# A message-passing layer on one core: coarser loads of edge features, destinations, empty rows and late rows, and the last three stores on another queue

## The chip, the core and the metric

The kernel runs on one core of a Trainium2 chip. It is written by hand, engine by engine: TensorE (PE; its weight loads are listed apart as PEld), VectorE (DVE), ScalarE (ACT), GpSimd (POOL) and SyncE (SP), which here does nothing but issue DMAs. The metric is the device time of one execution in microseconds (us); smaller is better. An execution's time is a little longer than the span from its first to its last instruction in the profile.

## What is computed

100,000 edges join 6,250 nodes of 128 numbers each. For each edge the rows of both ends and the edge's own 128 features are multiplied by a weight of 384 x 128, normalized over the 128 outputs, scaled, passed through relu, and summed at the edge's source node. The sum is added to the node's row and normalized again. The edges come sorted by destination, the sum goes by source.

```python
x = x + gnn(x, [src, dst], edge_attr); return layernorm(x)
# gnn:
msg_in = concatenate([x[row], x[col], edge_attr], axis=-1)   # row = src, col = dst
h = msg_in @ W + b                                           # W: 384 x 128
mu = mean(h, -1);  var = mean(square(h - mu), -1)
h = (h - mu) * rsqrt(var + 1e-5) * gamma + beta
out = segment_sum(relu(h), row, num_segments=6250)
```

## The kernel before

**Tiles, pieces, slots.** The edges are cut into 782 tiles of 128 (`TILES`), and four tiles (`PT = 4`) make a piece: 196 pieces. The main loop goes through the pieces in order, one piece per turn; a turn is called a slot here. The tiles are also divided into six splits of 168, 168, 168, 120, 80 and 78 tiles (`SPLITS`), each with a table `sorted` of its own in HBM.

**First half of a piece** (by destination). PE multiplies the four tiles of features `eT` (128 x 128 floats each) by the third part of the weight (L611), then adds the destination's part: a one-hot matrix `ohd`, which DVE makes from the piece's destinations `db` (L599), times a window `win` of a table of projected nodes that the kernel has written to HBM itself (L615). ACT copies the result from `hp` to one of eight buffers `hs` (`evict`, L623), and POOL scatters its 512 rows with four indirect DMAs (L641) to the places in `sorted` at which rows of the same block of source nodes lie together. The scatters of a slot are issued one slot later or more, each tied to one of the matmuls of that slot, so that they go out spread over it.

**Second half** (by source). 50 blocks of 125 nodes (`NB`, `BN`) make 25 pairs in every split. A split's pairs are worked through while the next split's pieces run (`work`, `class Pair`): SP loads the pair's rows from `sorted` (`load_pair`, L715, into `hl`, the late rows; four buffers), DVE makes a one-hot `ohe` from them (L733, `ones`), PE turns it, ACT copies `hl` on (L755, `seed`), PE adds the source's part (L772, `pick`), ACT squares (L781), DVE scales and cuts (L796, `scale`), PE sums (L805, `sums`), and DVE adds to `acc` (L810). A pair has k = 2 x 4, 2 x 3 or 2 x 2 tiles by split (8 in the first three splits, 6, 4 and 4 in the last three); `KMAX` is 8. The pair's load is issued six steps ahead of its `ones`, where four steps make one pair. In a slot stand 2.4 steps in the first splits, 3.3 in split 3, and 5 from slot 161 on: there five pairs fall on four slots. The last split's pairs come after the last piece, as `Unit`s of two pairs (one at the ends), and then the layernorm of the nodes and the stores of the result (`Unit.end`, L954).

**Empty rows.** `sorted` has room for a fixed number of rows per block, more than are used. The unused end of each is filled with a row that counts for nothing, before a split's scatters begin: `clear` (L232), one DMA for each pair of blocks, issued one or two per slot in the last 26 or 30 slots before the split (in split 0 in its own first slots).

**Order.** The order of PE, DVE, ACT and SP is written out by hand: each executes its instructions as the program's text issues them. SP's order in a slot q is: `edge_loads(ahead)` with `ahead` running up to q + 4 (features, L141, then destinations, L573, both for two slots in even slots only; three buffers of each), `edge_window(ahead)` (a register load and the window, L585; six buffers), `clear_pairs`, and the late rows that fall due in the slot's steps. Each waits in this order, so one that waits for a buffer holds up all behind it on SP. With three buffers of two slots, the features for q + 4 and q + 5 go to the buffer that q - 2 and q - 1 have used, so their load waits for the products of q - 1.

**The end.** After the last store there is a branch on a flag (L1268) to a general path that is not taken in this execution; the instructions of that path stand in the program behind it. A hint in the program (L1228) tells all engines ahead of time which way the branch goes.

Of the kernel before, what the change touches and what calls it, by code (L numbers as in the profile page):

```python
# [16 lines left out]
P = 128  # L17
D = 128
# [31 lines left out]
PG_AT = 192  # L50
XG = 4
ROW = 132
ACW = 130
# [13 lines left out]
def dram_ap(t, offset, ap):  # L67
    return bass.AP(tensor=t.tensor, offset=t.offset + offset, ap=ap)
# [16 lines left out]
def fast_path(ctx, tc, io, bad_d, found):  # L85
# [45 lines left out]
    dst0_i = setup.tile([1, BY_PE, PT * P], I32, name="dst0_i")  # L131
    DG = 2
    held = {}

    def edge_feats(q):
        t0 = q * PT
        g = min(DG, PIECES - q)
        eT = edge.tile([P, DG * PT * P], F32, name="eT", bufs=3)
        for n in ([(0, g)] if q else [(i, 1) for i in range(g)]):
            c0, c1 = n[0] * PT * P, min((n[0] + n[1]) * PT * P, (TILES - t0) * P)  # L140
            nc.sync.dma_start(eT[:, c0:c1], io["eT"][:, t0 * P + c0:t0 * P + c1])  # L141
        held["eT", q // DG] = eT

# [418 lines left out]
    def edge_loads(q):  # L562

        if q % DG or q >= PIECES:
            return
        t0 = q * PT
        g = min(DG, PIECES - q)
        if ("eT", q // DG) not in held:
            edge_feats(q)
        db = edge.tile([P, DG * PT * P], BF16, name="db", bufs=3)  # L570
        if q >= BY_PE:
            c1 = g * PT * P
            nc.sync.dma_start(  # L573
                db[:, :c1], dram_ap(drel_d, t0 * P, [[0, P], [1, c1]]))
        held[q // DG] = (held.pop(("eT", q // DG)), db)

# [12 lines left out]
    def edge_hot(q):  # L589
        if q >= PIECES:  # L590
            return
        m = min(PT, TILES - q * PT)
        c0 = q % DG * PT * P
        db = held[q // DG][1][:, c0:c0 + m * P]
        if q < BY_PE:
            db = psum.tile([P, PT * P], F32, name="sel", bufs=BANKS["sel"])
            nc.tensor.matmul(db, ones_h[0:1, :], drel0[0:1, q, :], start=True, stop=True)
        oh = edge.tile([P, PT * P], BF16, name="ohd", bufs=3)
        nc.vector.tensor_scalar(oh[:, :m * P], db, part_w, None, op0=ALU.is_equal)  # L599
        held["oh", q] = oh  # L600

    def edges(s, q):
        t0 = q * PT
        m = min(PT, TILES - t0)
        c0 = q % DG * PT * P
        eT = held[q // DG][0][:, c0:c0 + m * P]
        oh, win = held.pop(("oh", q)), held.pop(("win", q))
# [101 lines left out]
    loaded = {}  # L709

    def load_pair(s, p):

        k = 2 * SPLITS[s][1]
        pair = late["blk"].tile([P, KMAX, ROW], F32, name="hl", bufs=4)
        nc.sync.dma_start(flat(pair[:, :k, :]),  # L715
                          dram_ap(sorted_d[s], p * k * P * ROW, [[k * ROW, P], [1, k * ROW]]))
        loaded[s, p] = pair

    class Pair:
# [8 lines left out]
        def ones(self):  # L728

            blk, k = late["blk"], self.k  # L730
            self.hl = loaded.pop((self.s, self.p))
            self.ohe = blk.tile([P, KMAX, P], F32, name="ohe", bufs=4)
            nc.vector.tensor_tensor(self.ohe[:, :k, :],  # L733
                                    self.hl[:, :k, D:D + 1].to_broadcast([P, k, P]),
                                    row_bc(iota_p, k), op=ALU.is_equal)
# [83 lines left out]
    class Unit:  # L819
# [7 lines left out]
        def load(self):  # L827
            self.hl = late["blk"].tile([P, KMAX, ROW], F32, name="hl", bufs=4)
            for i in range(self.n):
                j0 = i * self.kp  # L830
                nc.sync.dma_start(flat(self.hl[:, j0:j0 + self.kp, :]),
                                  dram_ap(sorted_d[self.s], (self.p0 + i) * self.kp * P * ROW,
                                          [[self.kp * ROW, P], [1, self.kp * ROW]]))

# [110 lines left out]
        def end(self, last=False):  # L945
# [8 lines left out]
            nc.sync.dma_start(io["out"][:, self.b0 * D:(self.b0 + m) * D], flat(y))  # L954

# [147 lines left out]

    cleared = {s: 0 for s in range(n_split)}

    def clear_pairs(s, n):
        for p0 in range(cleared[s], min(cleared[s] + n, NB // 2)):
            i = clear(s, p0, 1, nc.sync)
            if s == 0:
                tc.declare_no_dep(i.ins, group="early", reason="see check_early")  # L1110
                tc.add_to_no_dep_group("clear", i.ins)
            cleared[s] = p0 + 1

# [111 lines left out]
    for i in range(1, n - 1):  # L1225
        tail(i)
    tc.no_sync_barrier()
    tc.mark_branch_hint_location("general", "LikelyTaken", engines=(  # L1228
        mybir.EngineType.PE, mybir.EngineType.DVE, mybir.EngineType.Activation,
        mybir.EngineType.Pool, mybir.EngineType.SP))  # L1230
    a, b, c, d = units[-4:]
# [29 lines left out]
def gnn_resnorm_kernel(ctx, tc, io):  # L1261
# [3 lines left out]
    with ExitStack() as inner:  # L1265
        found = []
        fast_path(inner, tc, io, bad_t, found)
    with tc.If(found[0] > 0, preferred_fallthrough_block=True, label="general"):  # L1268
        with ExitStack() as inner:
            general_path(inner, tc, io)  # L1270
# [233 lines left out]
```

## Time and profile before

| what | value |
|---|---|
| median of three runs | 1375.33 us (1369.01, 1375.33, 1378.67) |
| profiled execution | 1380.69 us, span 1378.9 us |
| mean granted TensorE clock | 0.857 of full speed |
| DMA | 128,052 packets, 247.22 MB, 179 GB/s over the span |
| of these on SP's and ACT's queue (q1) | 101,924 packets, 191.92 MB, 46.8% of 16 engines' span |
| POOL's scatters (q0) | 25,104 packets, 53.05 MB, 11.0% |

One execution was profiled, and all durations below are of that one; it was 5.4 us longer than the median. In a row of a group, `x782: 867/971/1241, 19.9 to 1274.6` means 782 instructions of min/median/max 867, 971 and 1241 ns, of which the first began at 19.9 us and the last at 1274.6 us of the span. A row of waits tells who waited for what, the total in us, how often, and the longest. In the timeline a row begins with the start and the time from the first to the last end of its group (`x2`: two instructions). An engine's name with a q behind it is its sequencer: `SPq` is SP issuing DMAs. Bytes: a load for two slots of features is 512 KB, of destinations 256 KB (read once for each of the 128 partitions), a pair's late rows are 528 KB, 396 KB or 264 KB, its empty rows 198 KB or 132 KB.

### The profile page before, as it was taken

What the parts mean: (1) busy time and instruction counts of PE and PEld (TensorE: products, weight loads), DVE (VectorE), ACT (ScalarE), POOL (GpSimd) and SP (SyncE); (2) the same over time, 40 slices, a digit from 0 to 9 for tenths busy, and PEclk for the clock granted to TensorE, in tenths of its full rate; (3) what the DMA queues carried; (4) which work ended last, traced back from release to release, by engine and by line L of the source; (5) the groups of instructions that cost most, each with busy time, mean ns of one, the idle gap of its engine ahead of it and who ended that gap; (6) DMA issues with size and microseconds to landing.
All of it is one profiled execution on the core that took longest, in us unless ns stands there. A gap on an engine that the chain in (4) does not pass through costs nothing. (4 is left out here: it accounts for less than half of the span.)

```text
span 1378.9 us, 27543 instructions
## 1 busy us (share of the span) xinstructions
PE 975.2 (71%) x8886; PEld 870.3 (63%) x8886; DVE 855.0 (62%) x2376; ACT 773.5 (56%) x3118; POOL 798.9 (58%) x835
## 2 busy tenths in 40 slices
PE   7457464345767676778777677778778787876895
PEld 5445453334666665777676667777778776765674
DVE  8573434524465656556575657678688867554797
ACT  4223232112555655564565557676778788665796
POOL 3656666666566665666565666566555555556054
PEclk9768687666888989878888899999999999988898
DMA  7758586455666655556656555665667655543332
GB/s 223 236 168 255 171 241 204 142 154 155 184 199 210 199 158 163 178 157 198 207 171 200 172 184 178 208 208 187 190 193 227 183 181 171 170 140 100 112 122 72
DMA packets 128052, 247.22 MB, mean 179 GB/s; under 512 B 47005, under 2 KB 61231, under 8 KB 127897
## 3 DMA queue, kind: packets, MB, share of 16 engines
q1 hardware_dynamic: 101924, 191.92, 46.8%
q0 software_dynamic: 25104, 53.05, 11.0%
q8 instruction: 71, 1.16, 0.4%
q14 instruction: 83, 0.68, 0.2%
q10 hardware_dynamic: 870, 0.40, 0.1%
HBM read 155.49 MB, written 89.80 MB: 178 GB/s over the span
## 5 line engine op out<-in xcount | busy, mean ns | idle before, releaser
L641 POOL DMA_INDIRECT sorted<-hs,place_i x782 | 760.4, 972 | 498.1 <-issue 210.6
L772 PE MATMUL sel<-xa,ohn 128*128 128x128 bf16 x2550 | 214.3, 232 | 174.9 <-issue 78.5
L781 ACT ACTIVATE sq<-sel 128x128 f32<-128x128 f32 x850 | 224.2, 280 | 158.9 <-PE sel L772 58.2
L772 PEld LDWEIGHTS <-ohn 128*128 128x128 bf16 x2550 | 174.8, 104 | 204.4 <-issue 174.7
L611 PE MATMUL hp<-w,eT 128*128 128x128 f32 x1564 | 258.3, 314 | 51.2 <-issue 37.9
L611 PEld LDWEIGHTS hp<-w,eT 128*128 128x128 f32 x1564 | 234.3, 225 | 83.2 <-issue 59.3
L805 PE MATMUL pa<-msg,ohe 128*128 128x130 f32 x1700 | 259.2, 308 | 24.1 <-issue 14.9
L623 ACT COPY hs<-hp 128x512 f32<-128x512 f32 x196 | 114.2, 583 | 288.7 <-issue 97.7
L805 PEld LDWEIGHTS pa<-msg,ohe 128*128 128x128 f32 x1700 | 236.4, 217 | 32.2 <-issue 19.0
L796 DVE SCALAR_TENSOR_TENSOR msg<-sel,rstd,cut 128x128 f32<-128x128 f32 x850 | 240.7, 345 | 8.0
L781 ACT ACTIVATION_READ_ACCUMULATOR sq<-sel 128x1 f32 x850 | 178.8, 210 | 0.0
L810 DVE TENSOR_TENSOR acc<-acc,pa 128x260 f32<-128x260 f32 x125 | 53.0, 424 | 201.0 <-PE pa L805 57.9
L733 DVE TENSOR_TENSOR ohe<-hl,beside 128x1024 f32<-128x1024 f32 (+2 forms) x125 | 131.4, 1052 | 23.3 <-PE sel L772 14.6
L749 ACT COPY ohn<-tr 128x1024 bf16<-128x1024 bf16 (+2 forms) x125 | 109.5, 876 | 37.9 <-PE pa L805 14.7
L755 ACT COPY sel<-hl 128x512 f32<-128x512 f32 (+1 forms) x225 | 127.9, 569 | 1.8 <-DVE msg L796 1.0
L599 DVE TENSOR_SCALAR ohd<-db,part_w 128x512 bf16<-128x512 bf16 x192 | 69.7, 363 | 72.1 <-remote 50.9
L615 PE MATMUL hp<-win,ohd 126*128 126x128 bf16 x782 | 88.5, 236 | 17.4 <-issue 15.4
L790 DVE RECIPROCAL rstd<-std 128x4 f32<-128x4 f32 (+1 forms) x225 | 38.6, 171 | 96.7 <-ACT std L784 45.2
L615 PEld LDWEIGHTS <-ohd 126*128 126x128 bf16 x782 | 69.0, 108 | 25.2 <-issue 20.9
L745 PE MATMUL tr<-ident_h,ohe 128*128 128x128 bf16 x850 | 75.5, 230 | 11.1 <-issue 9.4
L784 ACT ACTIVATE std<-ss,eps 128x4 f32<-128x4 f32 (+1 forms) x225 | 66.9, 297 | 7.3
L745 PEld LDWEIGHTS <-ohe 128*128 128x128 bf16 x850 | 57.7, 103 | 14.3 <-issue 14.2
(198 smaller groups left out, 1043.4 us busy)
## 6 DMA issues: line engine op xcount, KB each, us to landing
eT<-in_eT SPq DMA_DIRECT2D x96, 512.0 KB
hl<-sorted SPq DMA_DIRECT2D x75, 528.0 KB
db<-drel_d SPq DMA_DIRECT2D x96, 256.0 KB
sorted<-empty SPq DMA_DIRECT2D x100, 198.0 KB
hl<-sorted SPq DMA_DIRECT2D x50, 264.0 KB
sorted<-hs,place_i POOLq DMA_INDIRECT x782
hl<-sorted SPq DMA_DIRECT2D x25, 396.0 KB
sorted<-empty SPq DMA_DIRECT2D x50, 132.0 KB
```

The lines of the kernel that those rows point to most:

```text
L611: pe(nc.tensor.matmul(hp[:, j, :], eT[:, at], w[:, 2, :], start=j == 0, stop=False, skip_group_check=True), 4)
L615: pe(nc.tensor.matmul(hp[:, j, :], oh[:3 * WN, at], win[:3 * WN, :], start=False, stop=j == m - 1, skip_group_check=True))
L623: nc.scalar.copy(hs[:, :m, 0:D], hp[:, :m, :])
L641: i = nc.gpsimd.indirect_dma_start(out=sorted_d[s][:, :], out_offset=bass.IndirectOffsetOnAxis(ap=place_i[:parts, t:t + 1], axis=0), in_=h ...
L733: nc.vector.tensor_tensor(self.ohe[:, :k, :], self.hl[:, :k, D:D + 1].to_broadcast([P, k, P]), row_bc(iota_p, k), op=ALU.is_equal)
L745: pe(nc.tensor.transpose(tr[:, j, :], half[:, j0 + j, 1::2], ident_h))
L749: nc.scalar.copy(self.ohn[:, :self.k, :], self.tr[:, :self.k, :])
L755: nc.scalar.copy(self.sel[g][:, :m, :], self.hl[:, j0:j0 + m, 0:D])
L772: pe(nc.tensor.matmul(sel[:, j, :], self.ohn[:, j0 + j, :], xa[:, b, i * D:(i + 1) * D], start=False, stop=j == m - 1 and i == 2, skip_gro ...
L781: nc.scalar.activation(sq[:, j, :], self.sel[g][:, j, :], AF.Square, accum_out=ss[:, j:j + 1])
L796: nc.vector.scalar_tensor_tensor(self.msg[:, j0 + j, 0:D], self.sel[g][:, j, :], rstd[:, j:j + 1], cut, op0=ALU.mult, op1=ALU.max)
L805: pe(nc.tensor.matmul(self.pa[:, h, :], self.ohe[:, j, :], self.msg[:, j, :], start=(j == h), stop=(j == k - 2 + h)), 4)
```

## The change

Four kinds of transfers are cut anew, and three stores change queues. Nothing that is computed changes.

- **Features**: one load brings three slots instead of two (768 KB), in two buffers instead of three. The first group keeps two slots; the others begin at slots 2, 5, 8 and so on. So the group that begins at q + 4 goes to the buffer of q - 2, q - 1 and q, and its load, issued in slot q as before, waits for that slot's own products.
- **Destinations**: one load brings five slots instead of two (640 KB), two buffers instead of three; groups begin at 4, 9, 14 and so on. Groups of three and of five meet in every fifteenth slot.
- **Empty rows**: one DMA clears five pairs (two in split 0), when that many have fallen due.
- **Late rows**: where a pair has four tiles (the last two splits), one DMA brings two pairs, at the place where the first of the two is due; the buffer always had room for eight tiles.
- **Last stores**: the three stores of the last three units go on ACT's queue instead of SP's.
- **Branch**: the hint and a barrier ahead of it are gone, and the path that is taken is no longer the one that falls through.

```diff
@@
+EG, DG = 3, 5
+CLEAR = (2, 5, 5, 5, 5, 5)
...
-    DG = 2
     held = {}
+
+    def feats_from(q):
+        return 0 if q < 2 else q - (q - 2) % EG
 
     def edge_feats(q):
         t0 = q * PT
-        g = min(DG, PIECES - q)
-        eT = edge.tile([P, DG * PT * P], F32, name="eT", bufs=3)
+        g = min(EG, PIECES - q) if q else 2
+        eT = edge.tile([P, EG * PT * P], F32, name="eT", bufs=2)
         for n in ([(0, g)] if q else [(i, 1) for i in range(g)]):
             c0, c1 = n[0] * PT * P, min((n[0] + n[1]) * PT * P, (TILES - t0) * P)
             nc.sync.dma_start(eT[:, c0:c1], io["eT"][:, t0 * P + c0:t0 * P + c1])
-        held["eT", q // DG] = eT
+        held["eT", q] = eT
...
     def edge_loads(q):
-        if q % DG or q >= PIECES:
+        if q >= PIECES:
             return
-        t0 = q * PT
-        g = min(DG, PIECES - q)
-        if ("eT", q // DG) not in held:
+        if feats_from(q) == q and ("eT", q) not in held:
             edge_feats(q)
-        db = edge.tile([P, DG * PT * P], BF16, name="db", bufs=3)
-        if q >= BY_PE:
-            c1 = g * PT * P
+        if q >= BY_PE and (q - BY_PE) % DG == 0:
+            c1 = min(DG, PIECES - q) * PT * P
+            db = edge.tile([P, DG * PT * P], BF16, name="db", bufs=2)
             nc.sync.dma_start(
-                db[:, :c1], dram_ap(drel_d, t0 * P, [[0, P], [1, c1]]))
-        held[q // DG] = (held.pop(("eT", q // DG)), db)
+                db[:, :c1], dram_ap(drel_d, q * PT * P, [[0, P], [1, c1]]))
+            held["db", q] = db
...
+    def load_rows(s, p, n):
+        k = 2 * SPLITS[s][1]
+        rows = late["blk"].tile([P, KMAX, ROW], F32, name="hl", bufs=4)
+        nc.sync.dma_start(rows[:, :n * k, :].rearrange("p (n k) d -> p n (k d)", n=n),
+                          dram_ap(sorted_d[s], p * k * P * ROW,
+                                  [[k * ROW, P], [k * P * ROW, n], [1, k * ROW]]))
+        return rows
+
     def load_pair(s, p):
 
         k = 2 * SPLITS[s][1]
-        pair = late["blk"].tile([P, KMAX, ROW], F32, name="hl", bufs=4)
-        nc.sync.dma_start(flat(pair[:, :k, :]),
-                          dram_ap(sorted_d[s], p * k * P * ROW, [[k * ROW, P], [1, k * ROW]]))
-        loaded[s, p] = pair
+        n = KMAX // k
+        if p % n:
+            return
+        pair = load_rows(s, p, min(n, NB // 2 - p))
+        for i in range(n):
+            loaded[s, p + i] = pair, i * k
...
         def load(self):
-            self.hl = late["blk"].tile([P, KMAX, ROW], F32, name="hl", bufs=4)
-            for i in range(self.n):
...
+            self.hl = load_rows(self.s, self.p0, self.n)
...
-            nc.sync.dma_start(io["out"][:, self.b0 * D:(self.b0 + m) * D], flat(y))
+            queue = nc.scalar if last else nc.sync
+            queue.dma_start(io["out"][:, self.b0 * D:(self.b0 + m) * D], flat(y))
...
     cleared = {s: 0 for s in range(n_split)}
+    wanted = dict(cleared)
 
     def clear_pairs(s, n):
-        for p0 in range(cleared[s], min(cleared[s] + n, NB // 2)):
-            i = clear(s, p0, 1, nc.sync)
+        wanted[s] = min(wanted[s] + n, NB // 2)
+        while cleared[s] < wanted[s]:
+            m = min(CLEAR[s], NB // 2 - cleared[s])
+            if wanted[s] < cleared[s] + m:
+                break
+            i = clear(s, cleared[s], m, nc.sync)
...
-    tc.no_sync_barrier()
-    tc.mark_branch_hint_location("general", "LikelyTaken", engines=(
...
-    with tc.If(found[0] > 0, preferred_fallthrough_block=True, label="general"):
+    with tc.If(found[0] > 0, preferred_fallthrough_block=False):
```

Two places show how this moves instructions. The first is SP around the load of the features for piece 188, near the end of the pieces, where the slots hold most steps: eT are features, db destinations, win a window (with the register load and the address ahead of it), hl late rows. Before:

```order
L715 DMA hl_14253<-sorted4_75 128x528
L715 DMA hl_14312<-sorted4_75 128x528
L141 DMA eT_14329<-in_eT 128x1024
L573 DMA db_14331<-drel_d_70 128x1024
L581 TENSOR_LOAD base_c_177
L585 ISA
L585 DMA win_14336<-xb_d2_69 126x1x128
L715 DMA hl_14383<-sorted4_75 128x528
L715 DMA hl_14428<-sorted4_75 128x528
```

Now:

```order
L718 DMA hl_14022<-sorted4_75 128x2x528
L145 DMA eT_14039<-in_eT 128x1536
L583 TENSOR_LOAD base_c_177
L587 ISA
L587 DMA win_14044<-xb_d2_69 126x1x128
L718 DMA hl_14134<-sorted4_75 128x2x528
L575 DMA db_14140<-drel_d_70 128x2560
```

The two single loads of late rows ahead of the features have become one double load, and so have the two behind the window; the pair that the second of the single loads ahead of the features brought now comes with the load behind the window. The destinations have moved out of their place behind the features to one behind the late rows, since their groups no longer begin in the same slots.

The second place is ACT's end, from its last work on (sq and fstd belong to the last unit's variance). Before:

```order
L931 ACTIVATE sq,var<-y,total 128x128 x2
L934 ACTIVATE fstd<-var,eps 128x2
L1268 COMPARE_AND_BRANCH
L1300 DMA g_wn<-in_W 128x2x128
L1302 DMA g_we<-in_W 128x128
```

Now:

```order
L941 ACTIVATE sq,var<-y,total 128x128 x2
L944 ACTIVATE fstd<-var,eps 128x2
L965 DMA out<-y 128x512
L965 DMA out<-y 128x256 x2
L1280 COMPARE_AND_BRANCH
L1280 UNCONDITIONAL_BRANCH
```

Three stores stand between ACT's last work and the branch, and behind the branch there is now an unconditional one. The loads at L1300 and L1302, which followed the branch before, belong to the general path and are not executed. On SP the three stores are gone from the same place.

More of the change, by code (lines that the diff above doesn't have):

```diff
@@ L592, in edge_hot @@
         m = min(PT, TILES - q * PT)
-        c0 = q % DG * PT * P
-        db = held[q // DG][1][:, c0:c0 + m * P]
-        if q < BY_PE:
+        if q >= BY_PE:
+            c0 = (q - BY_PE) % DG * PT * P
+            db = held["db", q - (q - BY_PE) % DG][:, c0:c0 + m * P]
+        else:
             db = psum.tile([P, PT * P], F32, name="sel", bufs=BANKS["sel"])
@@ L604, in edges @@
         m = min(PT, TILES - t0)
-        c0 = q % DG * PT * P
-        eT = held[q // DG][0][:, c0:c0 + m * P]
+        q0 = feats_from(q)
+        c0 = (q - q0) * PT * P
+        eT = held["eT", q0][:, c0:c0 + m * P]
         oh, win = held.pop(("oh", q)), held.pop(("win", q))
@@ L730, in ones @@
             blk, k = late["blk"], self.k
-            self.hl = loaded.pop((self.s, self.p))
+            rows, j0 = loaded.pop((self.s, self.p))
+            self.hl = rows[:, j0:j0 + k, :]
             self.ohe = blk.tile([P, KMAX, P], F32, name="ohe", bufs=4)
@@ L1111, in clear_pairs @@
                 tc.add_to_no_dep_group("clear", i.ins)
-            cleared[s] = p0 + 1
+            cleared[s] += m
     ahead = 3
@@ L1226, in fast_path @@
         tail(i)
-    tc.no_sync_barrier()
-    tc.mark_branch_hint_location("general", "LikelyTaken", engines=(
-        mybir.EngineType.PE, mybir.EngineType.DVE, mybir.EngineType.Activation,
-        mybir.EngineType.Pool, mybir.EngineType.SP))
     a, b, c, d = units[-4:]
```

4 lines of the change are left out of this document (removed).

## The prediction

> **What bounds the kernel now.** First the page's head and busy shares:
>
> ```profile
> span 1378.9 us, 27543 instructions
> ...
> PE 975.2 (71%) x8886; PEld 870.3 (63%) x8886; DVE 855.0 (62%) x2376; ACT 773.5 (56%) x3118; POOL 798.9 (58%) x835
> ```
>
> No engine is full, but POOL is nearer its limit than its share says. Its scatters with first and last start, its largest row in the view of waits, and the pieces' products on PE:
>
> ```profile
> L641 POOL DMA_INDIRECT sorted<-hs,place_i x782: 867/971/1241, 19.9 to 1274.6; - x196
> POOL sorted L641 <- issue: 210.6, 535, 3.4
> L611 PE MATMUL hp<-w,eT x1564: 269/275/582, 13.9 to 1264.6; 128*128 128x128 f32 x196
> ```
>
> 782 scatters at 0.971 us are 759 us, and 210.6 us of pauses in which POOL waits for nothing shown make 970 us of the 1255 us from 19.9 to 1274.6. The other 285 us are waits on others: the scatters are tied to the products of their slot. PE goes through 196 pieces in 1250.7 us, so a slot is 6.4 us, and POOL, PE, ACT and DVE share it in a ring. No load stands in that ring. The view of one source line lists who waited for it (us in total, times). For the features (L141) that is the first row below, for the windows (L585) the next two, for the late rows (L715) the last; for the destinations (L573) the list is empty:
>
> ```profile
>   PEld hp L611: 0.8, 1
>   PE hp L615: 1.2, 1
>   PEld hp L611: 0.4, 1
>   PE hp L615: 0.6, 1
> ```
>
> Those are 3 us of 1379. The other way round SP waits often, at the feature loads for PE to be done with a buffer and at the late rows for ACT (SP's own waits, the three longest):
>
> ```profile
> SPq L715 <- ACT sel L755: 120.6, 35, 11.9
> SPq L141 <- remote: 96.7, 18, 10.1
> SPq L141 <- PE sel L772: 92.6, 15, 10.5
> ```
>
> So SP runs ahead until buffers stop it. Fewer issues buy nothing directly; what counts is whether a coarser load still comes in time.
>
> **The parts.** *Issues.* One feature issue, min/median/max ns:
>
> ```profile
> L141 SPq DMA_DIRECT2D eT<-in_eT x99: 3/348/1353, 1.7 to 1229.1; - x99
> ```
>
> The program has 756 DMAs on SP before and 529 on SP plus 3 on ACT after: feature loads 99 to 67, destinations 96 to 39, empty rows 150 to 38, late rows 150 to 127, and three stores moved. That is 224 issues less; at 0.348 us 78 us of SP's time. SP is waited for by nobody, so I take 0; the other end, a gain, is a rival below. The bytes stay the same.
>
> *Features, three slots in two buffers.* Leads are shortest near the end of the edges, where five pairs fall on four slots. SP, PE and DVE there, and the row of that stage in the table of windows (us; busy of PE, PEld, DVE, ACT, POOL; clock, DMA share, GB/s):
>
> ```profile
> 1182.09 0.34 SPq L141 DMA_DIRECT2D eT<-in_eT  x1
> 1182.48 0.80 SPq L573 DMA_DIRECT2D db<-drel_d  x1
> 1184.01 0.81 SPq L585 DMA_DIRECT2D win<-xb_d  x1
> 1184.92 4.62 SPq L715 DMA_DIRECT2D hl<-sorted  x2
> 1180.50 1.11 PE L611 MATMUL hp<-w,eT 128*128 128x128 f32 x8
> ...
> 1189.57 1.91 PE L611 MATMUL hp<-w,eT 128*128 128x128 f32 x8
> ...
> 1216.50 1.05 PE L611 MATMUL hp<-w,eT 128*128 128x128 f32 x8
> 1199.87 0.68 DVE L733 TENSOR_TENSOR ohe<-hl,beside 128x512 f32<-128x512 f32 x1
> 1000.00:1250.00 250.00, 194.68 (x2085) 183.34 (x2083) 178.44 (x535) 187.58 (x806) 140.30 (x145) 0.94 0.59 178
> ```
>
> The load at 1182.09 brings pieces 188 and 189. It waits for piece 183, whose products end at 1181.61, and goes out 0.5 us later. Piece 188 starts at 1216.50, 34.4 us after the issue. After the change the group is 188 to 190, its buffer held 182 to 184, so it waits for piece 184, done at 1191.48, and 25 us are left. At the stage's 178 GB/s, 768 KB (786,000 bytes) take 4.4 us. About 20 us of cover stay: cost 0. If that cover were gone, each group would cost up to a slot.
>
> *What stands behind that wait.* SP issues in order, so with the features every later issue of that slot waits for the current piece instead of the one before it: window, late rows, destinations, empty rows. The order on SP around the load for piece 188 stands under the change, before and now. Two late rows loads became one, and the pair of the second old load is now the first half of the load behind the features. Its old issue was at 1189.2 (the second of the two that end at 1189.54); DVE takes it at 1199.87. Now SP gets past the features at about 1191.9, past the window 2.3 us later (1182.09 to 1184.82, less some 0.4 for the destinations), so the late rows go out near 1194.2. Features and late rows are 1.33 MB; at 178 GB/s from 1191.9 on that is 7.4 us, and the latency on top is 1.5 us (under Start), so they land at 1200.8, 0.9 us late. At the 208 GB/s of the page's better slices it is 0.2 us early, at 157 GB/s 2.0 us late. About 36 slots run at this density, so 12 such places: between 0 and 12 x 2.0 = 24 us. A late load holds DVE, which is busy 178.4 of 250 us there, and behind it in its queue stand the scalings of the pair before, which PE's sums await. I take 4 us, a third of 12 x 0.9 = 11 us, since DVE idles 28% of the stage and can make up for the rest. In the earlier stages the slot holds fewer pairs and the late rows have more lead: 0.
>
> *Destinations, five slots.* 640 KB (655,000 bytes) behind 768 KB, in every fifteenth slot at the same place: 1.44 MB, 8.1 us and 1.5 of latency, wanted two slots (12.8 us) later: 0. Where DVE runs half a slot ahead it waits nothing to speak of; a whole slot ahead, 3 us at 13 places: upper end about 13 us if a third of them do.
>
> *Empty rows.* Five pairs are 1.0 MB at once instead of 0.2, 5.7 us at 178 GB/s on the queue, 25 such loads where 125 single ones stood. Nobody waits for them but the first scatter of a split, at least two slots later: 0, at worst 4 us once at the first split, where the last of them goes out behind features and destinations.
>
> *Start.* SP and PE in the first stretch, and the page's GB/s in 40 slices:
>
> ```profile
> 5.70 0.65 SPq L141 DMA_DIRECT2D eT<-in_eT  x1
> 9.54 2.85 SPq L376 DMA_DIRECT2D xb_d<-xb  x3
> 14.19 0.92 SPq L585 DMA_DIRECT2D win<-xb_d  x1
> 17.17 0.58 PE L615 MATMUL hp<-win,ohd 126*128 126x128 bf16 x4 [1.16 <-DMA win<-xb_d]
> GB/s 223 236 168 255 171 241 204 142 154 155 184 199 210 199 158 163 178 157 198 207 171 200 172 184 178 208 208 187 190 193 227 183 181 171 170 140 100 112 122 72
> ```
>
> The load at 5.70 grows by 262 KB, 1.2 us at the first slice's 223 GB/s, ahead of the stored table that the first window reads, and PE already waits 1.16 us for that window. Cost 0 to 1.2 us; I take 1. The last of the three stores goes out at some 12.05, and the window that needs it at 14.19: 2.1 us, of which 131 KB at 223 GB/s are 0.6, so 1.5 us of latency.
>
> *End.* Last stores and branches:
>
> ```profile
> 1368.83 5.14 SPq L954 DMA_DIRECT2D out<-y  x4
> L1268 SPq EVENT_SEMAPHORE  x8: 17/17/17, 1376.6 to 1377.2; - x8
> ...
> L1268 ACTq COMPARE_BRANCH  x1: 68/68/68, 1371.5 to 1371.5; - x1
> ...
> L1268 ACTq EVENT_SEMAPHORE  x1: 17/17/17, 1374.0 to 1374.0; - x1
> L1268 SPq COMPARE_BRANCH  x1: 70/70/70, 1374.0 to 1374.0; - x1
> L1500 SPq EVENT_SEMAPHORE  x14: 17/28/28, 1377.2 to 1378.8; - x14
> ```
>
> SP issues the last store until 1373.97, branches at 1374.0, comes back at 1376.6 and then goes through 22 waits one by one until the end at 1378.8. In ACT's order under the change, its last work stands before the stores, so nothing queues behind them but the branch. ACT issues at about 1373.65, branches at 1374.0, is back after its own 2.5 us (1371.5 to 1374.0) at 1376.5, while SP did its branch and most of its 22 waits since 1369.2. The 8 waits from 1376.6 to 1377.2 and some of the 14 behind them leave the path: a gain of about 1 us, between 0 and 1.5. The branch hint goes, and the jump to the end becomes an unconditional one: ACT lost 2.5 us and SP 2.6 us with the hint, so I price its loss at 0; a longer fetch would eat the gain. The Trainium skill, "DMA: Bandwidth & Descriptors", section "Issuing engines are not separate DMA queues", says that another issuing engine saves only the issue time; by that the gain is 3 x 0.35 us or less, which is no different.
>
> **Sum.** 0 + 4 + 0 + 0 + 1 - 1 = +4 us. The profiled execution took 1380.69 us (span 1378.9 and 1.8 outside), 5.4 above the median of 1375.33; 1384.7 against it, and on the scale of the median 1379.3. I forecast 1379.
>
> **Rivals.** *SP comes too late (slower).* If SP's lost slot isn't covered in the dense stage and where destinations meet features, the upper ends add: 24 + 13 + 4 + 1 - 1 = 41 us; half to two thirds of that, with what DVE's idle time swallows, is 23 us, 1398. It decides where the lead of the late rows behind a feature load falls under the 8.9 us that 1.33 MB take; in the place shown 8.0 us are left (1191.9 to 1199.87), so it has a real chance. Against it: when DVE and PE are late, the ring's next slot is late too, and SP has that time back.
>
> *Transfers get cheaper (faster).* ACT waits for scatters to land, and the DMA engines are busy 0.71 in the first stage:
>
> ```profile
> ACT hs L623 <- DMA sorted<-hs,place_i: 34.7, 19, 4.8
> 10.00:250.00 240.00, 136.90 (x869) 116.72 (x868) 116.65 (x253) 67.60 (x149) 144.99 (x149) 0.77 0.71 215
> ```
>
> If fewer, longer packets let scatters land sooner and half of the 34.7 us were on the ring, 17 us go: 1358. Against it: ACT is busy 68 of 240 us there, so its waits are mostly free. The Trainium skill, "Perfetto Trace Analysis", section "DMA Optimizations", holds larger transfers to be better, but also that splitting lets some start sooner where engines idle. By the first rule this case comes; by the second the slower one. The trace, with the DMA engines at 0.59 in the dense stage, bears out neither.
>
> *The coarser loads don't do what they say* can't be: the order shows them.
>
> **Numbers.** Within 1% means 1361.6 to 1389.1, about what a measurement of this kernel can tell from no change. Forecast 0.62 (its own range 1369 to 1388, the unknowns of the sum), slower rival 0.22, faster rival 0.16. The range 1357 to 1403 takes the forecast, most of the slower case and the faster one's price. Faster 0.16, same 0.62, slower 0.22.
>
> **What would show it.** Right: still nobody waits for L145 and L587, DVE's waits before the late rows' ohe grow to a few us in 1000 to 1250, POOL's scatters still at 0.97 us with about 6.4 us a slot, ACT's stores at the end and SP through its waits before them. Wrong: PE waiting for features; scatters ending 15 us later or earlier than 1274.6; ACT back from the last branch more than 3 us after it.

## The result, and the profile after

On the chip of the prediction the changed kernel took 1375.54 us (median of 22 runs, 1369.61 to 1381.38) against 1374.87 us of the kernel before: a ratio of 1.001, with a 95% interval of 0.9997 to 1.0023. The forecast was 1379 us and "within 1%". On three other chips, on which all experiments below ran, the kernel before takes only 1119 to 1122 us, and there the change costs 1.7% (run f2_after). So the number was right on the chip for which it was made; on the others "within 1%" would not have held. Most of this part is about why the same edit is free on one chip and not on the others.

The profile after, on the first chip. First the page's head and busy shares, then POOL's scatters and POOL's largest wait:

```profile
span 1373.9 us, 27120 instructions
...
PE 974.3 (71%) x8886; PEld 866.8 (63%) x8886; DVE 853.5 (62%) x2376; ACT 774.9 (56%) x3118; POOL 798.5 (58%) x835
```

```profile
L645 POOL DMA_INDIRECT sorted<-hs,place_i x782: 871/970/1276, 20.2 to 1267.8; - x196
POOL sorted L645 <- issue: 192.2, 512, 3.2
```

POOL's waits without a shown cause are 18 us shorter (210.6 before); little else has changed by more than the runs scatter (this profiled run took 1375.68 us, that of before 1380.69). Who waited for loads (us in total, times, longest), and the row of the dense stage in the table of windows:

```profile
DVE ohe L748 <- DMA hl<-sorted: 9.4, 4, 3.4
DVE ohd L602 <- DMA db<-drel_d: 2.7, 2, 1.5
1000.00:1250.00 250.00, 199.49 (x2103) 187.63 (x2103) 177.64 (x532) 191.36 (x825) 141.05 (x146) 0.92 0.57 185
```

Waits for late rows (hl) are new, 6.7 us of the 9.4 in the dense stage, as forecast. Yet POOL scattered no less there (146 scatters in those 250 us, 145 before).

The end has become longer. SP's instructions at the branch (L1280) and at the program's end (L1512), and the stores on ACT, after:

```profile
1365.29 2.23 ACTq L965 DMA_DIRECT2D out<-y  x3
L1280 SPq EVENT_SEMAPHORE  x8: 17/17/17, 1362.8 to 1369.4; - x8
L1280 SPq COMPARE_BRANCH  x2: 43/46/49, 1362.7 to 1369.5; - x2
L1512 SPq EVENT_SEMAPHORE  x14: 17/28/28, 1372.2 to 1373.8; - x14
```

SP passes its first branch at 1362.7, goes through its eight waits until 1369.4 (three of them for ACT's stores to land, the last of which was issued until 1367.5), takes a second branch at 1369.5 and goes on only at 1372.2. From the end of DVE's last instruction to the end of the span it is 6.73 us (1367.14 to 1373.88); before it was 5.28 us (1373.61 to 1378.89).

### The profile page after: what moved, and what is told of

Read it like the earlier page. It is cut to its first block, busy times and chain, and to the rows that moved or that the text cites. A ratio compares the mean times of both kernels' runs of the same rounds, so it can differ in the third digit from the quotient of the medians.

```text
span 1373.9 us, 27120 instructions
## 1 busy us (share of the span) xinstructions
PE 974.3 (71%) x8886; PEld 866.8 (63%) x8886; DVE 853.5 (62%) x2376; ACT 774.9 (56%) x3118; POOL 798.5 (58%) x835
## 5 line engine op out<-in xcount | busy, mean ns | idle before, releaser
L787 PE MATMUL sel<-xa,ohn 128*128 128x128 bf16 x2550 | 209.5, 231 | 148.8 <-issue 70.6
L615 PEld LDWEIGHTS hp<-w,eT 128*128 128x128 f32 x1564 | 237.6, 229 | 92.3 <-issue 38.9
L615 PE MATMUL hp<-w,eT 128*128 128x128 f32 x1564 | 263.6, 319 | 42.0 <-ACT hs L627 27.5
L820 PEld LDWEIGHTS pa<-msg,ohe 128*128 128x128 f32 x1700 | 230.2, 210 | 51.7 <-issue 36.2
L760 PE MATMUL tr<-ident_h,ohe 128*128 128x128 bf16 x850 | 79.7, 232 | 24.6 <-issue 24.5
```

What stands on the lines that cost most here:

```text
L615: pe(nc.tensor.matmul(hp[:, j, :], eT[:, at], w[:, 2, :], start=j == 0, stop=False, skip_group_check=True), 4)
L760: pe(nc.tensor.transpose(tr[:, j, :], half[:, j0 + j, 1::2], ident_h))
L787: pe(nc.tensor.matmul(sel[:, j, :], self.ohn[:, j0 + j, :], xa[:, b, i * D:(i + 1) * D], start=False, stop=j == m - 1 and i == 2, skip_gro ...
L820: pe(nc.tensor.matmul(self.pa[:, h, :], self.ohe[:, j, :], self.msg[:, j, :], start=(j == h), stop=(j == k - 2 + h)), 4)
```

## The experiments

All ratios are to the kernel before, measured beside it on the same chip. The experiments ran on three chips: those with e on one, those with f on a second, those with g on a third.

### Who pays at the end: the branch or the queue

e1_old_branch puts the hint, the barrier and the old branch back into the changed kernel; e2_stores_sp leaves the new branch and puts the three stores back on SP.

```diff
 # e1_old_branch, against the changed kernel
+    tc.no_sync_barrier()
+    tc.mark_branch_hint_location("general", "LikelyTaken", engines=(
...
-    with tc.If(found[0] > 0, preferred_fallthrough_block=False):
+    with tc.If(found[0] > 0, preferred_fallthrough_block=True, label="general"):
 # e2_stores_sp, against the changed kernel
-            queue = nc.scalar if last else nc.sync
+            queue = nc.sync
```

> The changed kernel with the branch of the kernel before (hint, barrier, taken path falls through); the last three stores stay on ACT. From the end of DVE's last instruction to the end of the span it was 5.3 us before and 6.8 us after the change. Theory: SP's jump of 2.7 us now stands behind its waits for the last stores to land, instead of beside them. With the old branch SP jumps while the stores are on their way: 3.9 to 4.3 us from DVE's last end, and a time 2 to 3 us below the changed kernel's. Rival: stores on ACT's queue are themselves later; then the end stays at 6 us or more.

> The changed kernel with the last three stores back on SP; the branch stays as changed. Theory (the place of the jump): 6.5 to 7 us from DVE's last end to the end of the span, as with the change, and the same time within 1 us. Rival (the stores on ACT's queue): about 5.3 us, as before the change.

Measured: e1_old_branch 1135.1 us, 1.0106 (1.009 to 1.0123), end 3.85 us after DVE's last instruction. e2_stores_sp 1138.12 us, 1.0148 (1.0124 to 1.0172), end 6.50 us. SP's rows at the end of e1_old_branch:

```profile
L1284 SPq COMPARE_BRANCH  x1: 70/70/70, 1126.3 to 1126.3; - x1
L1284 SPq EVENT_SEMAPHORE  x8: 17/17/17, 1129.3 to 1132.8; - x8
L1516 SPq EVENT_SEMAPHORE  x14: 17/28/28, 1132.9 to 1134.5; - x14
```

One branch, taken at 1126.3 while the last units are still being normalized; SP is back at 1129.3, and its waits for the stores end at 1132.8. In the changed kernel the jump of 2.7 us comes behind these waits. So it is the branch, not the queue: e2_stores_sp is 3.0 us slower than e1_old_branch on the same chip, and 2.65 us of that is its end. Stores on ACT with the old branch save 1.4 us against before (5.24 us there, in f1_before), as the prediction's end had it, and the new branch turns that into a loss. What surprised was the rest: both were over 1% slower than the kernel before, where 1.001 had been measured for the changed kernel. What differed was the chip.

### The same two kernels on another chip

f1_before and f2_after are the two kernels unchanged.

> The kernel before, unchanged, for its profile on the chip of these runs: another chip ran it in 1122.5 us where the first took 1375. Theory (on such a chip the ring is faster, the DMA queue is what the first 250 us lack, and single smaller loads stand it better): DVE waits for destinations under 10 us in all, against 32 to 37 us in the three versions of the changed kernel there, and SP's feature loads wait less for PE. Rival (the fast chip simply lacks DMA): 30 us or more of such waits here too.

> The changed kernel, unchanged. On the first chip it took 1.001 of the kernel before (0.9997 to 1.0023). Theory: where the kernel before takes about 1120 us it is 1.2 to 1.6% slower, as its versions with an old branch (1.1%) and with the stores on SP (1.5%) were; where that takes about 1375 us, within 0.3%. Rival (those versions are slower for what they take back): within 0.5% on either chip.

Measured: before 1119.66 us (its profiled run 1118.79); after 1139.02 us, 1.0174 (1.0157 to 1.0191). The theory of f2_after held. That of f1_before fell, and its rival held: DVE waits for destinations there, too, 31.1 us in 12 waits. The head of f1_before, its row of the windows from 250 to 650 us, and POOL's waits; then the same windows row of the first chip and of f2_after:

```profile
span 1117.0 us, 27543 instructions
...
PE 879.2 (79%) x8886; PEld 807.8 (72%) x8886; DVE 849.0 (76%) x2376; ACT 765.9 (69%) x3118; POOL 796.4 (71%) x835
```

```profile
250.00:650.00 400.00, 320.29 (x3374) 307.88 (x3375) 296.57 (x784) 283.65 (x1152) 304.26 (x315) 0.89 0.73 231
POOL sorted L641 <- issue: 108.1, 354, 0.4
POOL sorted L641 <- DMA sorted<-hs,place_i: 33.2, 109, 0.3
```

```profile
250.00:650.00 400.00, 266.06 (x2345) 241.17 (x2344) 228.36 (x564) 192.71 (x761) 247.61 (x255) 0.82 0.56 174
```

```profile
250.00:650.00 400.00, 315.20 (x3264) 302.48 (x3263) 289.79 (x757) 274.83 (x1119) 299.68 (x310) 0.88 0.73 226
```

DVE, ACT and POOL are busy for the same total time on either chip, to 1%; PE for 879 us instead of 975, at a clock of 0.89 instead of 0.82 in this stretch. POOL is what matters. On the fast chip it starts a scatter every 1.27 us (0.97 of work and 0.30 between two), 315 in 400 us, without a longer pause; POOL is busy 304 of 400 us and yet full. On the first chip it starts 255, with pauses of up to 3.4 us. In slots: four scatters at 1.27 us are 5.1 us, and that is a slot on the fast chip; on the first chip a slot takes 6.4 us. By this reading a stall of POOL is lost on the fast chips and can be made up on the first.

The start of scatter 4 x q marks slot q on POOL. With it every trace can be cut into stages (us; "pauses": scatters that start over 1.7 us after the one before, slots 20 to 160; "packets": the fewest of the scatters' DMA packets that started in any 12 us of these slots, taken in steps of half a us):

```
kernel             features  empty rows   to 20  20-160  160-194   rest   span   pauses  packets
f1_before          2 slots   1 pair       123.5   713.6    180.4   99.5  1117.0     0      206
f2_after           3         5, one DMA   125.1   723.4    189.0  100.8  1138.3     8      152
e1_old_branch      3         5, one DMA   127.6   723.7    185.4   97.9  1134.5    10      180
e2_stores_sp       3         5, one DMA   126.0   722.2    187.6  100.5  1136.3     6      170
e7_old_feats       2         5, one DMA   126.3   723.6    181.7  102.1  1133.7     6      174
f3_old_dests       3         5, one DMA   125.7   725.1    190.8   97.9  1139.5     9      174
f4_old_clears      3         1 pair       125.2   713.1    186.2   98.1  1122.7     0      197
g1_clears_only     2         5, one DMA   126.4   719.0    181.5   99.1  1126.0     7      177
g2_feats_only      3         1 pair       125.5   713.3    182.8   99.5  1121.1     0      201
g3_keep            2         1 pair       126.5   713.4    181.7   97.8  1119.3     0      209
g4_burst_singles   3         5, five DMAs 126.1   713.5    186.8   97.8  1124.2     0      205
e4_short_lead      2         1 pair       126.3   718.9    283.2   99.3  1227.7     4      213
before (chip 1)    2         1 pair       145.0   887.7    235.6  110.7  1378.9   150      160
after (chip 1)     3         5, one DMA   146.7   882.2    232.6  112.5  1373.9   146      130
```

f2_after is 21.3 us longer than f1_before: 1.6 at the start, 9.8 in slots 20 to 160, 8.6 in the dense stage, 1.3 at the end. The next experiments take these apart.

### Slots 20 to 160: the empty rows

f3_old_dests and f4_old_clears take one part back, on top of the old branch.

```diff
 # f3_old_dests, against e1_old_branch
-EG, DG = 3, 5
+EG, DG = 3, 2
-        db = edge.tile([P, DG * PT * P], BF16, name="db", bufs=2)
+        db = edge.tile([P, DG * PT * P], BF16, name="db", bufs=3)
 # f4_old_clears, against e1_old_branch
-CLEAR = (2, 5, 5, 5, 5, 5)
+CLEAR = (1, 1, 1, 1, 1, 1)
```

> The changed kernel with the old branch and with destinations as before (two slots a load, three buffers). On the fast chip the version with the old branch alone took 1.0106 and DVE waited 36.5 us for destinations, 34 us of it before 203 us. Theory (five slots' destinations in one load land too late for the first of the five): the waits for destinations fall under 8 us, and the time falls to 1.002 or less. Rival (the burst of empty rows fills the queue ahead of them): waits of 20 us or more stay, and the time stays at 1.007 or more.

> The changed kernel with the old branch and with the empty rows of one pair per DMA, as before. Theory (destinations): on the fast chip DVE's waits for destinations stay at 25 us or more and the time at 1.008 or more. Rival (bursts of empty rows): the waits fall under 12 us and the time to 1.004 or less.

Measured: f3_old_dests 1136.38 us, 1.0137 (1.01 to 1.0174), with 54.7 us of DVE's waits for destinations, more than with five slots. f4_old_clears 1124.19 us, 1.0049 (1.0026 to 1.0072), with 42.8 us of them. So I had looked at the wrong wait: DVE's waits for destinations stayed where the time fell, and the time stayed where the destinations were taken back. The theory of f3_old_dests fell and its rival held. In f4_old_clears neither did: the waits stayed, as the theory had it, and the time fell nearly as far as the rival had it (1.0049 against 1.004). The table shows what did go: 10 us of POOL's time in slots 20 to 160, and all its pauses. One of them in f2_after, POOL and then SP ahead of it (start, duration):

```profile
162.79 0.96 POOL L645 DMA_INDIRECT sorted<-hs,place_i  x1 [0.30 <-issue]
164.21 0.96 POOL L645 DMA_INDIRECT sorted<-hs,place_i  x1 [0.46 <-issue]
166.70 0.96 POOL L645 DMA_INDIRECT sorted<-hs,place_i  x1 [1.52 <-PE hp L615]
169.82 0.98 POOL L645 DMA_INDIRECT sorted<-hs,place_i  x1 [2.16 <-ACT hs L628]
171.10 0.97 POOL L645 DMA_INDIRECT sorted<-hs,place_i  x1 [0.30 <-PE sel L411]
```

```profile
151.95 0.65 SPq L575 DMA_DIRECT2D db<-drel_d  x1
153.34 0.84 SPq L587 DMA_DIRECT2D win<-xb_d  x1
154.23 0.42 SPq L240 DMA_DIRECT2D sorted<-empty  x1
154.71 0.44 SPq L700 DMA_DIRECT2D acc<-in_xblk  x1
155.26 3.27 SPq L145 DMA_DIRECT2D eT<-in_eT  x1
```

The releasers in brackets are guesses by time (they differ from pause to pause); what all eight pauses have in common is a DMA of five pairs 11 to 16 us earlier (here at 154.23). It is one of 990 KB each time: seven of the 14 such DMAs in these slots are followed by a pause (this one by two), none of the eight of 660 KB in the later splits. What the eight pauses last beyond the usual 0.30 us adds up to 9.3 us, nearly all of the stage's 9.8. g1_clears_only makes this one edit in the kernel before; g4_burst_singles keeps the bursts of e1_old_branch but issues each as five DMAs in a row.

```diff
 # g4_burst_singles, against e1_old_branch
-            i = clear(s, cleared[s], m, nc.sync)
...
+            for p0 in range(cleared[s], cleared[s] + m):
+                i = clear(s, p0, 1, nc.sync)
```

> The kernel before with empty rows of five pairs (two in split 0) per DMA, nothing else. Theory (a burst of 1 MB stops POOL's scatters some 12 us later, for 1 to 3 us, and POOL is the bound up to slot 160 where a slot takes 5.1 us): on the chip where the kernel before takes 1120 us POOL needs 723 us for slots 20 to 160 instead of 713, pauses over 1.7 us appear between scatters, and the time is 1.007 to 1.010 of before. On the chip of 1375 us: 1.000. Rival (single clears only helped because the old destinations or features were changed with them): 1.003 or less on the fast chip, too.

> The changed kernel with the old branch, whose bursts of empty rows are issued as five single DMAs one behind the other at the same place instead of one DMA. On the fast chip the version with one DMA took 1.0106 and POOL 723 us for slots 20 to 160. Theory (the bytes that come at once fill the queue): the same, 1.009 to 1.012. Rival (the shape of the one large DMA stops the scatters): pauses over 1.7 us vanish, 713 to 715 us, and 1.005 or less.

Measured: g1_clears_only 1128.25 us, 1.0084 (1.0067 to 1.0101), seven pauses and 719.0 us: the theory holds in time, but with only half of the 10 us of POOL's stage; the other half appears only where the other coarser loads stand beside it. (Another 2.9 us of its profiled run lie ahead of slot 20, where g3_keep with single pairs shows them, too.) g4_burst_singles 1127.8 us, 1.0093 (1.0067 to 1.0118): no pause, 713.5 us. In the traces the rival is right (one profile of each): it is the one large DMA that stops the scatters and not the bytes that come at once. In time it isn't settled: the median lies where the theory had it, 1.8 us above the profiled run (1125.97), whose other loss, in the dense stage, is f4_old_clears' too.

How the large DMA does it can be counted from the packets. In f2_after a feature load, destinations and five pairs of empty rows went out at 583.6, 584.0 and 586.0; in g4_burst_singles the same came from about 573 on. The scatters' packets that started in each microsecond from there (32 make one scatter, so POOL's pace of one in 1.27 us needs 25):

```
f2_after          584: 33  0  0  0  8 40 21 18 22 20 30 39   pause at 597.7 (2.5 us)
g4_burst_singles  573: 33  0  0  0  0 39 32 28 21 47 38 37   no pause
```

While features move, no scatter's packet starts for 3 to 4 us in both. Then five single DMAs let the scatters catch up, and one large DMA holds them at 18 to 22, below POOL's pace, for four microseconds, so that POOL runs out of room a few us later. The Trainium skill, "DMA: Bandwidth & Descriptors", section "Queues, rings and completion order", says that each DMA engine takes the queues in turn but drains a whole packet of descriptors from one before it goes on to the next. The microseconds without a scatter's packet agree with that in the two stretches shown (over all loads of 768 KB in slots 20 to 160 of f2_after such a gap is 2.5 us in the median, between 0.3 and 4.2); that the DMA of empty rows is cut into longer such packets than the single ones is an inference, which no run here shows.

What this room is, the traces show, though it took no part in any theory above. Each scatter signals its landing on one of eight semaphores, used in turn, and POOL waits on that semaphore before it uses it again: a scatter starts only when the one eight places before it has landed. Eight scatters at 1.27 us are 10.2 us. In slots 20 to 160 a scatter lands 4.5 us after its start in f1_before (median; at most 8.2), 4.8 in g4_burst_singles (at most 8.4) and 5.0 in f2_after (at most 10.9). In seven of the eight pauses of f2_after, and in all seven of g1_clears_only, that landing falls into the pause, and POOL's next scatter starts 0.75 to 0.78 us after it. (In the eighth, at 169.82, it doesn't; what held POOL there is open.) In the stretch of f2_after above, the scatter that started at 586.30 landed at 596.96; POOL's rows around it:

```profile
595.20 0.97 POOL L645 DMA_INDIRECT sorted<-hs,place_i  x1 [0.30 <-issue]
597.71 0.96 POOL L645 DMA_INDIRECT sorted<-hs,place_i  x1 [1.54 <-DMA sorted<-hs,place_i]
```

On the first chip eight scatters take two slots, 12.6 us on average. After the change the longest landing on record there took 9.8 us, and none of its 146 pauses holds such a wait. That fits with the coarser empty rows costing nothing there that can be seen.

### Slots 160 to 194: the features

e7_old_feats takes the features back in the changed kernel; g2_feats_only makes that one edit in the kernel before, where features now come as three slots in two buffers; g3_keep has features, empty rows and branch as before and keeps the rest of the change.

```diff
 # e7_old_feats, against the changed kernel
-EG, DG = 3, 5
+EG, DG = 2, 5
-        eT = edge.tile([P, EG * PT * P], F32, name="eT", bufs=2)
+        eT = edge.tile([P, EG * PT * P], F32, name="eT", bufs=3)
 # g3_keep: e7_old_feats, e1_old_branch and f4_old_clears together
```

> The changed kernel with features as before (two slots a load, three buffers). Both theories: DVE's waits for late rows, 9.4 us in 4 waits after the change, fall to 2 us or less. Theory as predicted: they cost the ring about 4 us, so the time falls by 3 to 5 us. Rival: DVE's idle time of 28% makes up for them, and the time stays within 1.5 us of the changed kernel's.

> The kernel before with features of three slots in two buffers, nothing else. Theory (late rows behind the later feature load): on the fast chip POOL needs 186 to 188 us for slots 160 to 194 instead of 181, all else stays, 1.004 to 1.006 of before; no more than 1.001 on the slow chip. Rival (what costs there is the pairs of late rows in one DMA): within 0.2% on either chip.

> The changed kernel with features, empty rows and branch as before; destinations of five slots, late rows of two pairs and stores on ACT stay. Theory (these three cost nothing, and the stores on ACT save 1.4 us at the end with the old branch): 0.997 to 1.001 of before on either chip, the end 3.8 to 4.1 us after DVE's last instruction. Rival (coarser destinations or late rows cost as well): 1.003 or more on the fast chip.

Measured: e7_old_feats 1135.56 us, 1.012 (1.0105 to 1.0135); g2_feats_only 1123.57 us, 1.0035 (1.0022 to 1.0048); g3_keep 1119.66 us, 1.0004 (0.9994 to 1.0014). DVE's waits for late rows between 820 and 1045 us (us in total, times, longest), in f2_after and in g2_feats_only:

```profile
DVE ohe L748 <- DMA hl<-sorted: 7.6, 5, 3.2
```

```profile
DVE ohe L740 <- DMA hl<-sorted: 5.9, 6, 2.2
```

In g2_feats_only POOL needs 182.8 us for the stage, less than the 186 to 188 expected, and the time lies between theory and rival. With two slots of features a load (f1_before, e7_old_feats, g3_keep) the list has no such row there (only one wait of about 1 us behind the pieces, at the units). POOL's time in the stage follows: 180.4 to 181.7 us without these waits, 182.8 with the features alone, 185.4 to 190.8 where the features meet late rows of two pairs (with f3_old_dests the longest). Against f4_old_clears, g3_keep differs in the features alone: 4.5 us of the stage, and 1.0004 instead of 1.0049. e7_old_feats lost the dense stage's 7 us and kept the 10 us of the empty rows; DVE's waits for late rows fell only from 27.7 us to 21.0, and not under 2 us as expected, since some 14 us of either are one wait for the very first late rows, which f1_before has, too.

e4_short_lead goes on in the direction of the change: the kernel before, with two feature buffers of two slots.

```diff
 # e4_short_lead, against the kernel before
-        eT = edge.tile([P, DG * PT * P], F32, name="eT", bufs=3)
+        eT = edge.tile([P, DG * PT * P], F32, name="eT", bufs=2)
```

> The kernel before with two feature buffers of two slots instead of three, nothing else: SP waits in slot q for the products of q + 1, two slots later than before and one later than with the change. Theory (the lead of the late rows is what counts, and it has an end): in the dense stage the late rows go out 6 to 8 us later than they are wanted in every second slot; DVE waits for them in 15 to 18 places, and the time grows by 30 to 90 us. Rival (loads never bound this ring, SP gets its time back): within 5 us of the kernel before.

Measured: 1231.25 us, 1.0983 (1.0957 to 1.1009), or 109 us more; 103 of them in slots 160 to 194 (283.2 us instead of 180.4). DVE's waits for loads in the whole run:

```profile
DVE ohe L733 <- DMA hl<-sorted: 130.7, 34, 11.4
DVE ohd L599 <- DMA db<-drel_d: 103.3, 41, 9.3
```

That is more than the 30 to 90 us expected, with 34 waits for late rows instead of 15 to 18; and destinations, which stand behind the features too, are waited for 103.3 us (31.1 in f1_before). Its four pauses of POOL lie behind 829 us, and no scatter there took over 7.7 us to land, so they aren't those of the empty rows. So what counts is indeed SP's lead for what stands behind the features. The change takes one slot of it in every third slot and costs 2 to 10 us of the stage; one slot more, in every second, costs 109.

## Why the prediction was right, and where not

- **Issues, 0.** Right. 224 issues less gained nothing anywhere: g3_keep, which keeps the coarser destinations and late rows, is at 1.0004. The rival by which transfers get cheaper didn't come either: on the first chip ACT's waits for scatters did fall, from 34.7 us to 17.5, and the time stayed. Nor did scatters land sooner (in slots 20 to 160 after 3.2 us before and 3.4 after in the median there, 4.5 and 5.0 in f1_before and f2_after).
- **Features and late rows, +4 us, between 0 and 24.** Right in mechanism, with fewer places (3 to 6 instead of 12) and more at each (1.0 to 2.2 us on average). On the first chip DVE waited the 6.7 us and the ring lost nothing that can be seen; on the others POOL's dense stage grew by 2.4 us with the features alone and by 5 to 10 where late rows of two pairs stand behind them. The 4 us that the sum took for them did not come on the first chip. That DVE makes up for its waits while POOL has pauses of its own is a reading of these stages; no run tests it.
- **Destinations, 0.** Right: taking them back (f3_old_dests) gave nothing, 1.0137 against 1.0106, on two chips. On the first chip DVE waited for them twice, 2.7 us in all.
- **Empty rows, 0, at worst 4 us once.** Wrong as a step, and the largest one on the fast chips: 10 us in slots 20 to 160, and 9 us as the only edit. The prediction asked who waits for the empty rows (nobody) and not who shares the DMA engines with them: POOL's scatters do. On the first chip the step's number held, and that was luck: the step had not asked how late a scatter may land. There eight scatters take 12.6 us on average, and the longest landing on record took 9.8.
- **Start, +1 us.** Right where it was read: on the first chip the first window goes out at 15.21 us instead of 14.19, and PE's first product with it starts at 18.24 instead of 17.17 (+0.3 us from f1_before to f2_after). What is left of it by slot 20 isn't resolved, since that stage scatters by 2 us among kernels that start alike.
- **End, -1 us.** Wrong in sign: +1.45 us (6.73 instead of 5.28). The moved stores do give the gain of the step (1.4 us), but only with the old branch. The step looked at the hint and priced its loss at 0; what it missed is the place of the unconditional branch. The order on ACT showed that branch, but not that on SP it stands behind the waits for the stores, so that its 2.7 us no longer lie beside the stores' landing. The prediction's own sign, SP through its waits before ACT's stores, failed with it: SP's waits end at 1369.4, 1.9 us after the last of these stores was issued.
- **The slower rival.** Its mechanism is real (e4_short_lead), its condition was put too high: it was to come with a lead under 8.9 us, 8.0 were expected in the place shown, and still DVE waited in only three places of the dense stage on the first chip. On the fast chips the time grew by 19 us, 4 or 5 of them by this rival, and about 9 by a mechanism that I had not named.

On the first chip the sum of +4 us met a measured +0.7 (interval -0.4 to +3.2), so it is a little high, and that it comes so close is in part luck: the 4 us for the late rows didn't show, and the end's -1 was +1.45.

What stays open: the change costs 19.4 us on the fast chips (1139.02 against 1119.66). By separate runs 9 go to the empty rows alone (6 where they are taken back from e1_old_branch) and 4 to the features alone; less the 1.4 us that the stores save, that is 12, and e1_old_branch loses 12 to 13. The other 7 lie between e1_old_branch and f2_after, which differ in the branch alone but ran on two chips. The end explains 2.9 of them by the traces (3.85 us against 6.79), and the two runs on one chip agree with that (3.0 us); the remaining 4 are not explained. Nor is the end of e7_old_feats, 8.19 us after DVE's last instruction, where one gap of 1.7 us lies between two of SP's last waits. Why the first chip's ring is slower than its PE's busy time and clock account for (96 us more busy time, but 255 us more in all) was not tried. All experiments ran on the fast chips; that the same parts cancel or vanish on the first is read from the two traces there.

No version here beats both kernels. g3_keep, the best, saves 1.4 us at the end by the trace and cannot be told from the kernel before by its time.

## What to carry to other kernels

When a transfer is made larger, ask who shares the DMA engines with it, not only who waits for it: here a transfer that nobody waits for stopped the one engine that was full. An engine's busy share doesn't tell that it is full; the spacing of its instructions does (0.97 us of work every 1.27 us, at 76% busy). Such an engine may also have a limit on how many transfers it keeps open (here eight scatters), and it shows only when one of them lands late. And a change that costs nothing on one chip may only lie in that chip's slack: look at what covers it there, and at what a faster ring would show.

## What was not expected of the hardware

- The same program took 1375 us on one chip and 1119 to 1122 on three others, with the same busy time of DVE, ACT and POOL to 1%, and 975 against 879 us of PE's.
- On the fast chips a DMA of 990 KB of empty rows can stop another queue's scatters some 11 to 16 us later, for 0.7 to 3 us (seven of 14 in f2_after); the same bytes in five DMAs didn't (6 to 10 pauses in a run against none). POOL then waits for the scatter eight places back, which took up to 11 us to land instead of 4.5.
- A taken branch at the end costs SP 2.5 to 3.0 us before its next instruction in the runs read (1369.5 to 1372.2 after the change, 1126.3 to 1129.3 in e1_old_branch, with the hint), wherever it stands; the program decides whether that lies beside the last stores or behind them.
